# Expert choice: pooling the chosen tokens by rows fetched from DRAM instead of by products over all tokens

## The chip, the cores and the metric

The kernel runs on one core of one Trainium2 chip. The metric is device time in microseconds (us) of one execution; before the change it is 8233.12 us, the median of three runs (8232.96 to 8242.14).

The engines are named as in the profile: PE (TensorE matmul; PEld is its weight load), DVE (VectorE), ACT (ScalarE), POOL (GpSimd), SP (SyncE, which here only issues DMAs).

## The reference, cut to what matters

A network of four layers (each a token mixer and a feed-forward part) works on `x` of shape 4 x 128 x 64 x 64: four images of 4,096 tokens with 128 channels, all in float32. The change touches the feed-forward part of layers 1 and 2, an "expert choice" mixture of 64 experts in which each expert chooses its 8 best tokens of each image:

```
x = layernorm(tokens)                                   # over the 128 channels
logits = einsum('bsd,ed->bse', x, gate_w) + gate_b
probs = softmax(logits, axis=1)                         # over the 4,096 tokens
vals, idx = top_k(probs.transpose(0, 2, 1), 8)          # for each image and expert
gathered = take_along_axis(x, flat_idx)                 # the chosen tokens' rows
pooled = einsum('bked,bke->bed', gathered, topv)        # weighted sum of the 8 rows
h = gelu(einsum('ebd,edh->ebh', [pooled, 1], weight1))  # 128+1 -> 512
out = einsum('ebh,eho->ebo', [h, 1], weight2)           # 512+1 -> 128
outputs.at[b, flat_idx].add(topv * out)                 # back to the chosen tokens
```

The result is added to the tokens. Per layer, `weight1` and `weight2` hold 64 experts x 2 x 128 x 512 values, 32 MB.

## The kernel before

The whole `x` stays in SBUF as `xs`, 128 channels on the partitions, 4 images of 4,096 tokens along the free dimension. Eight phases run one after the other; `expert_choice(net, 1)` is the fourth and `expert_choice(net, 2)` the sixth. Between them lies a convolution, ahead of the first a deformable convolution, behind the second an attention.

On PE, ACT, DVE and POOL the instructions of a phase run in the order in which the program writes them (`manual_schedule(engines=ORDERED)`). SP is not among those: the order of its DMAs is set by the framework's planner, and each DMA waits for its data and for the buffer that it fills. A buffer pool that takes the place of another one waits for the old one's last users.

One expert stage has three parts.

Part A works on two pairs of images (`p` 0 and 1; the partitions hold 64 experts of the pair's first image and 64 of its second). `stat` makes the variances: a centring product of each chunk of 512 tokens, its square on ACT, and products that add the squares up. `scales` and `inverted` make the inverse deviations, and `turn_scales` transposes them so that each token's lies on its partition (`turned`). `logits` fills `chosen[p]`, 128 x 4,096. `largest` finds the eight largest of each row on DVE (MAX8), `exponentials` makes exp(logit - largest) and its sum (`totals`) on ACT. `choose` marks the eight places by overwriting them with a number (MATCH_REPLACE8) and then keeps the exponentials there and zero elsewhere; so `chosen[p]` becomes a sparse matrix of weights.

The pooling then takes 64 steps of 128 tokens. A step (`pool`, `gather`) transposes the 128 tokens of both images (two PE transposes, `moe_pt`), transposes the weights by a product with a diagonal matrix `diags[p]` that divides by the sum, brings the result to SBUF on ACT and DVE (`moe_tt`, with the tokens' scale `turned`), and adds the product of weights and tokens to `moe_acc`. `centre` takes the mean over channels off by one more product and writes `pooled`. The logits of pair 1 and its choice are interleaved with the first steps:

```
for n in range(PAIRS * NT):
    p, t = divmod(n, NT)
    tt = pool(p, t, p == 0 and t > 10)
    if before:
        gather(*before)
```

Part B goes through 16 groups of four experts: `first` (128 to 512), `turn` (transpose, bias, gelu), `second` (512 to 128), `hand` (collects the rows of all experts). A group's weights are two DMAs of 1 MB (`load`). Three groups' weights are fetched during part A into the pool `early`; the pool `late`, for two more, is opened when part A's pools are closed:

```
weights = [load(g) for g in range(EARLY)]
...
tc.tile_pool(name="moe_w_b", bufs=LATE) as late,
```

Part C multiplies the experts' results by `chosen` (64 products of 128 x 512) and adds them to `xs` on DVE.

The profile holds another phase that does what the change adds, in its own sizes. The deformable convolution writes rows of 512 bytes to a DRAM table (`dcn_table<-dcn_xt`, 64 partitions, 1,024 rows a DMA) and fetches rows of 2 KB by place, 128 for each indirect DMA (`dcn_g<-dcn_table,dcn_idx`). The involution writes zeros to the border of an image in DRAM (`inv_image<-inv_zero`): 128 rows of 1.8 KB a DMA, which don't start on round addresses.

Of the kernel before, what the change touches and what calls it, by code (L numbers as in the profile page):

```python
# [19 lines left out]
I32 = mybir.dt.int32  # L20
# [890 lines left out]
def expert_choice(net, layer):  # L911
# [9 lines left out]

    tc, nc, ins = net.tc, net.nc, net.ins
# [5 lines left out]
    PAIRS = B // 2  # L928
    EARLY, LATE = 3, 2
    GONE = -3.0e38  # L930
    w1, w2 = ins[f"L{layer}_ffn_weight1"], ins[f"L{layer}_ffn_weight2"]
    with ExitStack() as ctx:
        keep = ctx.enter_context(tc.tile_pool(name="moe", bufs=1))
# [11 lines left out]

        pooled = keep.tile([P, E, CG], F32, name="moe_pooled")
        nc.gpsimd.memset(pooled, 0.0)
        acts = [keep.tile([P, NH, EG, CG], F32, name=f"moe_act{i}") for i in range(2)]
        for t in acts:
            nc.gpsimd.memset(t, 0.0)  # L950
# [9 lines left out]
        cgate = keep.tile([D, E], F32, name="moe_cgate")  # L960

# [10 lines left out]
        with (  # L972
# [5 lines left out]
            def bank(tag, name):  # L978
                return ps.tile([P, CH], F32, name=f"moe_{name}", tag=tag, bufs=3 if tag in "ab" else 1)
# [3 lines left out]
            def stat(p, j):  # L983

                if j == 0:
                    stats[p] = (bank("pv", "pv"), [])
                pv, squares = stats[p]
                pd = bank("a", "pd")
                nc.tensor.matmul(pd, net.cent, net.chunk(2 * p + j // NCH, j % NCH), start=True, stop=True)
                sq = sb.tile([P, CH], F32, name="moe_sq", tag="moe_sq", bufs=6)  # L990
                nc.scalar.activation(sq, pd, AF.Square)
                squares.append(sq)
                if j % 4 == 1 and j > 4:
                    variances(p, j // 4 - 1)
# [56 lines left out]
            tops, exps, diags = {}, {}, {}  # L1051

            def largest(p):
                top = sb.tile([P, 8], F32, name="moe_top", tag="moe_top")
                nc.vector.max(out=top, in_=chosen[p])
                neg = sb.tile([P, 1], F32, name="moe_neg", tag="moe_neg")
                nc.vector.tensor_scalar_mul(neg, top[:, 0:1], -1.0)
                tops[p] = (top, neg)

            def exponentials(p):  # L1060
                exps[p] = sb.tile([P, N], F32, name="moe_exp", tag="moe_exp", bufs=1)
                nc.scalar.activation(exps[p], chosen[p], AF.Exp, bias=tops[p][1], accum_out=totals[p])

            def choose(p):
                lg = chosen[p]
                nc.vector.match_replace(out=lg, in_to_replace=tops[p][0], in_values=lg, imm_value=GONE)
                nc.vector.reciprocal(totals[p], totals[p])
                nc.vector.scalar_tensor_tensor(
                    out=lg, in0=lg, scalar=GONE, in1=exps[p], op0=ALU.is_equal, op1=ALU.mult
                )  # L1070
                diags[p] = sb.tile([P, P], F32, name="moe_diag", tag="moe_diag")
                nc.vector.tensor_scalar_mul(diags[p], net.ident, totals[p])

            accs = {}

            def pool(p, t, on_scalar):

                if t == 0:
                    accs[p] = bank("acc", "acc")[:, 0 : 2 * E]
                pt = bank("b", "pt")[:, 0 : 3 * P].rearrange("p (n c) -> p n c", c=P)  # L1080
                tok = slice(t * P, (t + 1) * P)
                for i in range(2):
                    nc.tensor.transpose(pt[:, 1 + i, :], net.xs[:, 2 * p + i, tok], net.ident)
                nc.tensor.matmul(pt[:, 0, :], chosen[p][:, tok], diags[p], start=True, stop=True)
                tt = sb.tile([P, 3, P], F32, name="moe_tt", tag="moe_tt", bufs=3)
                scale = turned[p][:, :, t // 4, t % 4]
                nc.scalar.copy(tt[:, 1:3, :], pt[:, 1:3, :])
                if on_scalar:
                    for i in range(2):
                        half = slice(i * E, (i + 1) * E)  # L1090
                        nc.scalar.activation(tt[:, 0, half], pt[:, 0, half], AF.Copy, scale=scale[:, i : i + 1])
                else:
                    nc.vector.tensor_mul(
                        tt[:, 0, :].rearrange("p (i e) -> p i e", e=E),
                        pt[:, 0, :].rearrange("p (i e) -> p i e", e=E),
                        scale.unsqueeze(2).to_broadcast([P, 2, E]),
                    )
                return tt

            def gather(p, t, tt):  # L1100
                for i in range(2):
                    half = slice(i * E, (i + 1) * E)
                    nc.tensor.matmul(
                        accs[p][:, half],
                        tt[:, 1 + i, :],
                        tt[:, 0, half],
                        start=t == 0 and i == 0,
                        stop=t == NT - 1 and i == 1,
                    )

            def centre(p):
                raw = sb.tile([P, 2 * E], F32, name="moe_raw", tag="moe_raw")
                nc.scalar.copy(raw, accs[p])
# [20 lines left out]
            for j in range(5):  # L1134
                stat(1, j)
            for c in range(NCH):
                logits(0, c)
            turn_scales(0)
            largest(0)
            for j in range(5, 10):  # L1140
                stat(1, j)
            exponentials(0)
            choose(0)
            for j in range(10, 2 * NCH):
                stat(1, j)
            scales(1)
            inverted(1)
            before = None
            for n in range(PAIRS * NT):
                p, t = divmod(n, NT)  # L1150
                tt = pool(p, t, p == 0 and t > 10)
                if before:
                    gather(*before)
                    if before[1] == NT - 1:
                        centre(before[0])
                before = (p, t, tt)
                if p == 0:
                    if 2 <= t < 2 + NCH:
                        logits(1, t - 2)
                    if t == 10:  # L1160
                        turn_scales(1)
                        largest(1)
                    if t == 17:
                        exponentials(1)
                        choose(1)
            gather(*before)
            centre(1)
# [3 lines left out]
        with (  # L1171
# [6 lines left out]
            def first(g):  # L1178
# [3 lines left out]
                ph = ps.tile([P, HID], F32, name="moe_ph", tag="ph")  # L1182
                for j in range(EG):
                    nc.tensor.matmul(
                        ph[j * CG : (j + 1) * CG], pooled[:, e0 + j, :], t1[:, j, :], start=True, stop=True
# [5 lines left out]
            def turn(g, hs):  # L1191
# [3 lines left out]
                for i in range(NH):  # L1195
                    nc.tensor.transpose(pt[:, i].rearrange("p j k -> p (j k)"), hs[:, i:HID:NH], net.ident)
                hid = sb.tile([P, NH, EG, B], F32, name="moe_hid", tag="hid")
                nc.vector.tensor_add(
                    hid,
# [3 lines left out]
                act = acts[g % 2]  # L1203
                nc.scalar.activation(act[:, :, :, 0:B], hid, AF.Gelu)
                return act

            def second(g, act, t2):
                po = ps.tile([P, D], F32, name="moe_po", tag="po")
                for i in range(NH):
                    for j in range(EG):  # L1210
                        nc.tensor.matmul(
                            po[j * CG : (j + 1) * CG],
# [8 lines left out]

# [727 lines left out]
```

## Time and profile before

| | us |
|---|---|
| median of three runs | 8233.12 |
| profiled execution | 8237.43 |
| its span (first to last instruction) | 8235.6 |
| stage of layer 1: first weight load to first product of the next phase | 2794.9 to 3056.3 |
| stage of layer 2: first DMA to first product of the next phase | 3375.8 to 3633.4 |

The mean granted clock of PE is 0.969 of full speed. The profile page gives busy time by engine, the span in 40 slices, the chain of work that ended last, and the costliest groups of instructions. Besides it, the trace answers for any stretch of the span: instructions in order of time, the chain in order of time, who waited for whom, busy time and granted clock by window, and DMA packets by window. Times in those lines are microseconds from the span's start; a line of the timeline has the start, the busy time, engine, line, operation, tiles, count, and in brackets the idle time before it with what ended it. "DMA share" is the mean busy share of the core's 16 DMA engines.

### The profile page before, as it was taken

Reading aid. Unit: us, or ns where it says so; the run is one execution under the profiler, and the core shown is the slowest. Engines: PE = TensorE matmul, PEld = TensorE weight load, DVE = VectorE, ACT = ScalarE, POOL = GpSimd, SP = SyncE. Lnnn points to the kernel's source line nnn. Section 1 sums busy time; section 2 is a strip of 40 time slices with the busy share of each in tenths; the row PEclk is TensorE's granted clock in tenths of the full one; section 3 lists DMA queues with packets and bytes.
Section 4 is the critical chain, followed back from the end, with each engine's and each line's share of the span. In section 5 each row is a group of like instructions: output and inputs, shape, how many; then the busy total and the mean of one; then the engine's idle time right before and its main releaser. Section 6 shows DMA issues by size and latency. Waiting matters only on the chain.

```text
span 8235.6 us, 146123 instructions
## 1 busy us (share of the span) xinstructions
PE 7626.6 (93%) x59726; PEld 3315.2 (40%) x59726; DVE 5525.9 (67%) x8715; ACT 3801.2 (46%) x7248; POOL 5253.5 (64%) x2925
## 2 busy tenths in 40 slices
PE   8999986777877889989999999999999999999899
PEld 2222243555555454443444344443444434444333
DVE  7888856888888632237767667766677667677155
ACT  4444433444444430323555555555555555555511
POOL 5989804777777400004888688887888878888700
PEclk9999998999999999988999999999999999999999
DMA  6434206877877430032554445544445445555400
GB/s 182 96 73 96 49 1 164 248 224 234 249 209 209 145 136 0 32 144 47 111 110 100 106 101 108 109 106 103 106 100 111 105 103 107 108 105 109 99 22 23
DMA packets 299127, 944.82 MB, mean 115 GB/s; under 512 B 41876, under 2 KB 114644, under 8 KB 240596
## 3 DMA queue, kind: packets, MB, share of 16 engines
q0 software_dynamic: 142848, 671.18, 34.6%
q1 hardware_dynamic: 155604, 264.26, 11.3%
q8 instruction: 469, 7.68, 0.4%
q14 instruction: 206, 1.69, 0.1%
HBM read 466.78 MB, written 65.88 MB: 65 GB/s over the span
## 4 chain that ended last, share of the span: by engine, by line
PE 57%; DVE 2%; issue 1%; DMA 1%; ACT 1%; POOL 0%; SPq 0%; DVEq 0%; ACTq 0%; POOLq 0%
PE att_pv L1552 15%; PE att_sc L1639 13%; PE att_mx L1496 11%; PE att_sc L1540 5%; PE conv_po L1306 3%; PE top_po L1852 3%; PE top_pw L1828 1%; DVE att_most L1507 1%; DMA moe_w<-in_L_ffn_weight 1%; PE att_sc L1469 0%; PE att_sc L1583 0%; PE top_po L1850 0%; PE att_sc L1600 0%; PE att_mx L1394 0%; PE att_sc L1430 0%
## 5 line engine op out<-in xcount | busy, mean ns | idle before, releaser
L1571 POOL TENSOR_TENSOR att_acc<-att_acc,att_ex 128x2048 f32<-128x2048 f32 x640 | 2902.0, 4534 | 638.5 <-ACT att_ex L1640 619.2
L1507 DVE TENSOR_REDUCE att_most<-att_mx 128x2 f32<-128x1024 f32 x2016 | 2461.8, 1222 | 1070.5 <-PE att_mx L1496 992.6
L1640 ACT ACTIVATE att_ex<-att_sc 128x512 f32<-128x512 f32 x4096 | 2222.9, 595 | 1771.4 <-PE att_sc L1639 1491.4
L1639 PE MATMUL att_sc<-att_q,att_k 32*128 32x512 f32 x8192 | 2455.7, 606 | 0.0
L1496 PE MATMUL att_mx<-att_k,att_q 32*128 32x512 f32 x8064 | 2292.2, 647 | 13.0 <-DVE att_parts L1519 10.8
L1540 PE MATMUL att_sc<-att_rows,att_ones_b 32*128 32x256 bf16 (+1 forms) x6144 | 1502.2, 306 | 4.7 <-ACT att_ex L1640 4.7
L816 POOL DMA_INDIRECT dcn_g<-dcn_table,dcn_idx x1152 | 1100.7, 955 | 436.9 <-DMA dcn_g<-dcn_table,dcn_idx 122.2
L1552 PE MATMUL att_pv<-att_ex,att_vals 128*32 128x256 f32 x16384 | 1309.8, 391 | 0.0
L1496 PEld LDWEIGHTS att_mx<-att_k,att_q 32*128 32x128 f32 x8064 | 610.9, 185 | 867.1 <-issue 707.6
L409 POOL TENSOR_TENSOR inv_prod<-inv_seen,inv_prod 128x512 f32<-128x512 f32 (+1 forms) x672 | 837.5, 1273 | 94.1 <-ACT inv_prod L408 94.1
L411 DVE SCALAR_TENSOR_TENSOR inv_prod<-inv_pk,bspan,inv_seen 128x512 f32<-128x512 f32 (+1 forms) x1120 | 774.6, 743 | 140.2 <-PE inv_pk L398 139.9
L1552 PEld LDWEIGHTS att_pv<-att_ex,att_vals 128*32 128x32 f32 x16384 | 322.5, 108 | 1318.9 <-issue 1300.8
L1639 PEld LDWEIGHTS att_sc<-att_q,att_k 32*128 32x128 f32 x8192 | 818.3, 183 | 10.7 <-issue 8.3
L830 ACT ACTIVATE dcn_one<-dcn_g,dcn_w 128x128 f32<-128x128 f32 x1152 | 457.5, 401 | 790.9 <-DMA dcn_g<-dcn_table,dcn_idx 787.6
L857 PE MATMUL dcn_pt<-ident,dcn_sum 128*128 128x128 f32 x2304 | 516.7, 308 | 242.6 <-DVE dcn_sum L841 241.8
L408 ACT ACTIVATE inv_prod<-inv_pk,bspan 128x512 f32<-128x512 f32 (+1 forms) x672 | 436.1, 682 | 503.8 <-PE inv_pk L398 503.8
L856 PE MATMUL dcn_pt<-ident,dcn_one 128*128 128x128 f32 x2304 | 482.9, 293 | 93.2 <-ACT dcn_st L873 81.1
L856 PEld LDWEIGHTS dcn_pt<-ident,dcn_one 128*128 128x128 f32 x2304 | 397.3, 203 | 305.7 <-issue 137.8
L398 PE MATMUL inv_pk<-inv_red,wtap 32*96 32x512 f32 (+1 forms) x3584 | 511.4, 636 | 7.4 <-DMA inv_seen<-inv_image 7.4
L857 PEld LDWEIGHTS dcn_pt<-ident,dcn_sum 128*128 128x128 f32 x2304 | 371.6, 203 | 322.1 <-DVE dcn_sum L841 321.0
L833 DVE TENSOR_SCALAR dcn_part<-dcn_g,dcn_w 128x128 f32<-128x128 f32 x1152 | 405.8, 352 | 122.5 <-DMA dcn_g<-dcn_table,dcn_idx 89.8
L420 PE MATMUL inv_out<-inv_prod,inv_fold 96*32 96x512 f32 (+1 forms) x3584 | 478.0, 605 | 8.5 <-DVE xs L428 8.5
(339 smaller groups left out, 7090.2 us busy)
## 6 DMA issues: line engine op xcount, KB each, us to landing
att_sum<-att_ex POOLq DMA_DIRECT2D x320, 1024.0 KB, 7.2
inv_seen<-inv_image SPq DMA_DIRECT2D x256, 266.0 KB
moe_w<-in_L_ffn_weight SPq DMA_DIRECT2D x64, 1024.0 KB
dcn_table<-dcn_xt SPq DMA_DIRECT2D x64, 512.0 KB
att_sum<-att_ex SPq DMA_DIRECT2D x32, 1024.0 KB
att_sum<-att_acc POOLq DMA_DIRECT2D x32, 1024.0 KB, 7.2
dcn_g<-dcn_table,dcn_idx POOLq DMA_INDIRECT x1152, 3.7
inv_image<-inv_rows SPq DMA_DIRECT2D x32, 304.0 KB
```

The lines of the kernel that those rows point to most:

```text
L409: nc.gpsimd.tensor_mul(of, view, of)
L411: nc.vector.scalar_tensor_tensor(out=of, in0=as_shape(pk[0:m], of), scalar=by, in1=view, op0=ALU.add, op1=ALU.mult)
L816: nc.gpsimd.indirect_dma_start(out=g, out_offset=None, in_=rows, in_offset=bass.IndirectOffsetOnAxis(ap=idx[:, j + i, k : k + 1], axis=0),)
L856: nc.tensor.matmul(out, one_, net.ident, start=i == 0, stop=False)
L857: nc.tensor.matmul(out, s, net.ident, start=False, stop=i == 3)
L1496: nc.tensor.matmul(pm[i] if alone else pm[:, i, :], q[r, t * P : (t + 1) * P], ks[r, kc * CH : (kc + 1) * CH], start=True, stop=True,)
L1507: nc.vector.tensor_reduce(most[:, 2 * half : 2 * half + 2, kc], pm, AX.X, ALU.max)
L1540: nc.tensor.matmul(pe[:, cols], ones_b[r], lows[g][r, cols], start=cols.start == 0, stop=False)
L1552: nc.tensor.matmul(block["pv"][r, cols], vals[b][:, t, r], ex[:, h, cols], start=t == 0 and half == 0, stop=t == NT - 1 and half == 1,)
L1571: nc.gpsimd.tensor_add(block["acc"], block["acc"], ex)
L1639: nc.tensor.matmul(pe, ks[r, t * P : (t + 1) * P], qs[c][r], start=False, stop=True)
L1640: nc.scalar.activation(ex[:, h, :], pe, AF.Exp)
```

## The change

The products over all tokens are taken out. In their place the tokens' rows are written to DRAM: `rows` transposes a chunk of 512 tokens of one image on PE, ACT copies it to `moe_xt`, POOL adds the tokens' scale as a 129th column, and SP writes 512 rows of 516 bytes to `moe_table`, one table for each pair of images. `largest` also finds the places of the eight largest (`max_index`), moves those of the second image up by 4,096 and turns them into integers. `ask` fetches the j-th chosen row of all 128 (image, expert) pairs by one indirect DMA on POOL. `pool` makes for each j a diagonal matrix of share times scale and adds up the eight rows by eight products with them; `centre`'s work stands at its end.

`choose` is split into `mark` and `choose`: pair 0's run during the second half of the rows, pair 1's during part B, since only part C needs them now. `turn_scales(0)` moves ahead of the logits, `exponentials(0)` behind `scales(1)`. `logits(1, ...)` are interleaved with the rows.

In part B, `pooled` and the activations hold four columns an expert instead of 32 with zeros between, and the PSUM tiles `phs` and `pos` are fixed and set to zero once by DVE. Two POOL memsets (`pooled`, `acts`) are gone.

```diff
+    K, ROW = 8, P + 1
+        tables = [dram.tile([2 * N, ROW], F32, name=f"moe_table{p}") for p in range(PAIRS)]
...
-        pooled = keep.tile([P, E, CG], F32, name="moe_pooled")
-        nc.gpsimd.memset(pooled, 0.0)
-        acts = [keep.tile([P, NH, EG, CG], F32, name=f"moe_act{i}") for i in range(2)]
-        for t in acts:
-            nc.gpsimd.memset(t, 0.0)
+        pooled = keep.tile([P, E, B], F32, name="moe_pooled")
...
+        def mark(p):
+            lg = chosen[p]
+            nc.vector.match_replace(out=lg, in_to_replace=tops[p], in_values=lg, imm_value=GONE)
+
+        def choose(p):
+            lg = chosen[p]
+            nc.vector.scalar_tensor_tensor(
+                out=lg, in0=lg, scalar=GONE, in1=exps, op0=ALU.is_equal, op1=ALU.mult
+            )
...
+            def rows(b, c):
+                p, i = divmod(b, 2)
+                pt = bank("b", "pt")
+                for t in range(4):
+                    tok = slice((4 * c + t) * P, (4 * c + t + 1) * P)
+                    nc.tensor.transpose(pt[:, t * P : (t + 1) * P], net.xs[:, b, tok], net.ident)
+                xt = sb.tile([P, 4, ROW], F32, name="moe_xt", tag="moe_xt", bufs=5)
+                nc.scalar.copy(xt[:, :, 0:P], pt.rearrange("p (t d) -> p t d", d=P))
+                nc.gpsimd.tensor_copy(xt[:, :, P], turned[p][:, i, c, :])
+                first = i * N + c * CH
+                nc.sync.dma_start(tables[p][first : first + CH, :].rearrange("(t p) r -> p t r", p=P), xt)
...
             def largest(p):
...
+                nc.vector.max_index(out=place, in_max=top, in_values=chosen[p])
+                row = sb.tile([P, K], F32, name="moe_row", tag="moe_row")
+                nc.vector.tensor_copy(row, place)
+                nc.vector.tensor_scalar(row, row, behind, None, op0=ALU.add)
+                places[p] = sb.tile([P, K], I32, name="moe_idx", tag="moe_idx")
+                nc.vector.tensor_copy(places[p], row)
...
+            def exponentials(p, neg):
+                nc.scalar.activation(exps, chosen[p], AF.Exp, bias=neg, accum_out=totals[p])
+                shares[p] = sb.tile([P, K], F32, name="moe_share", tag="moe_share")
+                nc.scalar.activation(shares[p], tops[p], AF.Exp, bias=neg)
+
+            def ask(p, j):
+                if j == 0:
+                    asked[p] = sb.tile([P, K, ROW], F32, name="moe_asked", tag="moe_asked")
+                nc.gpsimd.indirect_dma_start(
+                    out=asked[p][:, j, :],
+                    out_offset=None,
+                    in_=tables[p],
+                    in_offset=bass.IndirectOffsetOnAxis(ap=places[p][:, j : j + 1], axis=0),
+                )
+
+            def pool(p):
                 nc.vector.reciprocal(totals[p], totals[p])
+                nc.vector.tensor_scalar_mul(shares[p], shares[p], totals[p])
+                acc = bank("acc", "acc")[:, 0 : 2 * E]
+                for j in range(K):
+                    diag = sb.tile([P, P], F32, name="moe_diag", tag="moe_diag", bufs=4)
+                    nc.vector.tensor_scalar(
+                        diag, net.ident, shares[p][:, j : j + 1], asked[p][:, j, P : P + 1],
+                        op0=ALU.mult, op1=ALU.mult,
+                    )
+                    nc.tensor.matmul(acc, asked[p][:, j, 0:P], diag, start=j == 0, stop=j == K - 1)
...
+            turn_scales(0)
             for c in range(NCH):
                 logits(0, c)
-            turn_scales(0)
-            largest(0)
-            for j in range(5, 10):
-                stat(1, j)
-            exponentials(0)
-            choose(0)
-            for j in range(10, 2 * NCH):
+            neg = largest(0)
+            for j in range(5, 2 * NCH):
                 stat(1, j)
             scales(1)
+            exponentials(0, neg)
             inverted(1)
...
+            for n in range(2 * NCH):
+                rows(*divmod(n, NCH))
+                if n == 5:
+                    turn_scales(1)
+                if n > 5 and n % 2 == 0:
+                    logits(1, n // 2 - 3)
+            for n in range(2 * NCH):
+                rows(2 + n // NCH, n % NCH)
+                if n < 6 and n % 2 == 0:
+                    logits(1, 5 + n // 2)
+                if n == 5:
+                    neg = largest(1)
+                    mark(0)
+                    choose(0)
+                if 5 < n < 6 + K:
+                    ask(0, n - 6)
+            exponentials(1, neg)
+            for j in range(K):
+                ask(1, j)
+            pool(0)
+            pool(1)
...
+            phs = [ps.tile([P, HID], F32, name=f"moe_ph{i}", bufs=1) for i in range(2)]
+            pos = [ps.tile([P, D], F32, name=f"moe_po{i}", bufs=1) for i in range(2)]
+            for t in phs + pos:
+                nc.vector.memset(t, 0.0)
...
+                if g == 4:
+                    mark(1)
+                if g == 7:
+                    choose(1)
```

## The prediction

> **What bounds the kernel now.** I read the page first, then the chain of waits over the two expert stages, then windows inside them, then the DMA rows that come nearest to the new transfers.
>
> ```profile
> PE 7626.6 (93%) x59726; PEld 3315.2 (40%) x59726; DVE 5525.9 (67%) x8715; ACT 3801.2 (46%) x7248; POOL 5253.5 (64%) x2925
> ...
> PE 57%; DVE 2%; issue 1%; DMA 1%; ACT 1%; POOL 0%; SPq 0%; DVEq 0%; ACTq 0%; POOLq 0%
> ```
>
> The busiest engine by share and the chain agree on PE, but both average eight stages, most of them untouched here. The chain, cut to the second expert stage (layer 2), starts, lasts, what:
>
> ```profile
> 3421.96 0.59 PE moe_pr L1022 x4
> ...
> 3429.98 3.81 ACT moe_exp L1062 x2
> 3433.81 4.49 DVE moe_chosen L1066 x2
> 3438.37 4.39 DVE moe_chosen L1068
> 3442.96 3.26 DVE moe_rstd L1016
> ...
> 3535.44 0.49 PE moe_pc L1115 x2
> ...
> 3543.23 14.60 DMA moe_w<-in_L_ffn_weight
> ```
>
> The stage runs from 3375.8 to 3633.4 us and has three parts. Part A (statistics, logits, choice, pooling) ends with the centring product at 3535.9. Part B streams the 26 loads of 1,024 KB of weights that were not fetched earlier; the chain there is nearly all DMA. Part C adds the result to `xs` on DVE until 3633.4. Inside A, the exponentials, the marking, the choice and the reciprocal follow one another for 18 us while the token loop stands still. The same stage windowed (us, PE, PEld, DVE, ACT, POOL busy, granted clock, DMA share, GB/s):
>
> ```profile
> 3446.00:3476.00 30.00, 29.58 (x148) 14.39 (x148) 8.39 (x19) 12.77 (x25) 0.00 (x0) 0.87 0.00 1
> 3490.00:3536.00 46.00, 44.82 (x359) 41.72 (x358) 16.96 (x38) 21.95 (x70) 0.00 (x0) 0.95 0.01 1
> 3558.00:3574.00 16.00, 12.22 (x152) 7.31 (x152) 1.54 (x6) 2.53 (x6) 0.00 (x0) 0.89 1.05 406
> ```
>
> The first two windows are the token loop: PE is busy for nearly all of it, in 64 steps of three transposes or products and two small products. DMA is empty. In the third, DMA carries 406 GB/s and sets the pace. SP issues the first late weight load at 3535.96, when the centring product ends, so B can't start before A ends, and what A loses the whole stage loses. Layer 1 has the same shape: turning of the scales at 2841.8, centring ended at 2959.0.
>
> **The change, part by part (layer 2, then layer 1).** Removed: the loop from 3443 to 3535.9, less eight logits steps that stay. Added: 32 row blocks (four transposes, an ACT copy, a POOL column, a store of 512 rows of 516 B), 16 gathers, 16 diagonal products.
>
> *Until the rows.* The turning of the scales moves ahead of the logits at the same price. From 3422.5, PE has 11 statistics products of 0.93 us and four groups of variances of 1.0: 14.2, to 3436.7. No exponentials or DVE stand in it any more. ACT then takes the root (0.69), a table (1.28), the exponentials (3.71 + 0.19) and a small one (0.2): 3442.8. Copy 0.58, and 1.4 from issue to first data (the deformable stage's table stores were issued from 1275.96 and reached their rate near 1277.4): 3444.8.
>
> *The stores* are what I expect to bound the rows. The nearest rows are 512-byte stores of the deformable stage (1280 to 1315 us) and unaligned stores of 1.8 KB (24 to 28 us):
>
> ```profile
> DMA packets 12343, 6.24 MB, mean 178 GB/s; under 512 B 194, under 2 KB 12342, under 8 KB 12342
> ```
>
> ```profile
> DMA packets 885, 1.45 MB, mean 362 GB/s; under 512 B 97, under 2 KB 885, under 8 KB 885
> ```
>
> The first kept 97.4% of 16 engines busy: 0.974 x 35 x 16 / 12343 = 44 ns a packet. The second, 98.1%: 3.92 x 16 / 885 = 71 ns, or 80 if the 97 short packets are free; a line from 512 B (44) to the weights' 2 KB (81) gives 76 there, so starting off a boundary cost at most 4 ns. A 516-byte packet costs at least 44 and at most the 80 of the longer unaligned one; I take 47, by the nearer row. 16,384 x 47 / 16 = 48.1 us.
>
> [...]
>
> PE beside it: 29 more blocks of 0.86, eight logits of 2.01, 0.6 for the scales: 41.6, to 3484; covered by the stores. ACT has 32 x 0.58 and 8 x 1.3. The eight gathers of pair 0 share the engines: 65 gathers of 256 KB took 72.4% of 80 us (2700 to 2780), 0.89 us each; a quarter of the bytes costs 0.23 to 0.89, so 1.8 to 7.1, I take 3.5 (per-row costs don't shrink with the bytes). Stores end at 3444.8 + 48.1 + 3.5 = 3496.4, and land 1.0 later (the first table buffer's four stores ended near 1288.7, ACT was let go at 1289.7).
>
> *The tail.* `ask(1)` waits on POOL for the last store; nothing of the stage is queued behind it there. (`ask(0)` comes six blocks after its pair's last store and should find it landed; if not, the POOL columns of the last ten blocks queue behind it, and their stores on SP, which has only the late weight loads after them.) Its pace is in the first gathers of the deformable stage, and in ACT's wait for the first of them:
>
> ```profile
> 1331.70 1.22 POOL L816 DMA_INDIRECT dcn_g<-dcn_table,dcn_idx  x1 [83.39 <-DMA dcn_table<-dcn_zero]
> 1333.22 1.10 POOL L816 DMA_INDIRECT dcn_g<-dcn_table,dcn_idx  x1 [0.30 <-issue]
> 1334.63 0.95 POOL L816 DMA_INDIRECT dcn_g<-dcn_table,dcn_idx  x1 [0.30 <-issue]
> ```
>
> ```profile
> 1335.46 0.40 ACT L830 ACTIVATE dcn_one<-dcn_g,dcn_w 128x128 f32<-128x128 f32 x1 [4.28 <-DMA dcn_g<-dcn_table,dcn_idx]
> ```
>
> The eighth starts 1.52 + 1.41 + 5 x 1.25 = 9.2 after the first and lands 3.76 later: 13.0, to 3510.4. Diagonal 0.28, product 0.43, copy 0.27, centring 0.49, hops: 1.6, to 3512.0. Against 3535.9 that is 23.9 us. Layer 1 is the same 580.1 earlier: 2931.9 against 2959.0, 27.1. Sum 51.0.
>
> *The clock.* Today's stall is followed by PE at half speed; these are windows of layer 1 and layer 2:
>
> ```profile
> 2870.00:2880.00 10.00, 10.00 (x32) 4.15 (x28) 1.67 (x3) 2.84 (x6) 0.00 (x0) 0.50 0.00 0
> 3449.00:3452.00 3.00, 3.00 (x9) 0.58 (x8) 0.12 (x1) 0.58 (x1) 0.00 (x0) 0.50 0.00 0
> ```
>
> 0.50 lasted 14 us in layer 1 and 6 in layer 2: 7 + 3 us of PE time. The new wait for the exponentials is 4 to 6 us, about as long, and PE has little slack in the first 22 blocks. Between 0 and 10; I take 6.
>
> [...]
>
> *At nothing.* `max_index` (4.4 us as MATCH_REPLACE8, plus five small operations of 0.15) stands under 14 us of statistics on PE and ACT; bare, 5. `largest(1)`, `mark(0)`, `choose(0)` are 19 us on DVE from 3478, then 4.1 on ACT: 3501, with `pool(0)` behind it, before the last gathers at 3510; bare, 5. `mark(1)` and `choose(1)` delay DVE by 4.4 each in B, but five groups of weights are allocated, some 20 us of DMA queued; bare, 9. Four PSUM memsets (about 1.6) and fewer weight columns lie under the same stream. The POOL memsets removed were on no chain. B's 67 us of DMA and C don't change.
>
> Profiled time 8237.4 (span 8235.6 and 1.8 around it), less 45; the runs' median is 8233.1, so 8188. Ends: 44 ns, cheap gathers, no slow clock give 51 + 6 + 3.4 = 60, 8173; 56 ns (a quarter of the way from 47 to 80), dear gathers, 10 of clock give 51 - 18 - 7 - 10 = 16, 8217.
>
> **The rivals.**
> *PE-paced rows.* The 44 ns came from 64 partitions; if 128 store faster, PE sets the end at 3484, plus 4.2 to land, plus 14.6: 3503, and DVE's own chain holds it at 3506. Gain 30 + 33 - 6 = 57 or slightly more: 8174. Against it: the 1.8 KB stores, from 128 partitions, lie on the same line.
>
> *Dear stores (slower).* One mechanism: a 516-byte row costs what a long packet does, because it is cut in two or written in parts at both ends. At 80 ns, 33 x 1.024 = 33.8 more in each stage: 45 - 68 = -23, 8256. It decides from 47 + 22 = 69 ns, where the gain is zero. Against it: the involution's reads of 8.5 KB show as packets over 8 KB, not cut, and unaligned 1.8 KB cost 4 ns extra. For it: no row here has 516 B.
>
> *Slow clock throughout.* The deformable stage's transposes, waiting for stores as these would, ran at 0.57 to 0.60 between 1285 and 1305. At 0.72 (layer 1's slice from 2860 to 2890) the 41.6 us become 58, the stores land 7 later and the time is 8197; at 0.50 they become 83, 33 later, 8247; from 0.55 down there is no gain. Against it: PE is busy for 60% or more here, not 30%.
>
> That stores to one table queue behind each other's landing would cost 32 x 2 us a stage; the deformable stage stores to one table at 97% busy, which excludes it.
>
> **How the numbers follow.** Forecast 0.66 (0.06 of it within the band), PE-paced 0.12, dear stores 0.14 (0.03 within), slow clock 0.08 (0.03 faster, 0.02 within, 0.03 slower). 0.2% is 16.5 us and about what a measurement can tell from no change. Faster 0.60 + 0.12 + 0.03 = 0.75, same 0.06 + 0.03 + 0.02 = 0.11, slower 0.14. The range from 8168 to 8226 leaves out most of the dear stores and half of the slow clock.
>
> **What would show it.** Right: from the rows on, DMA near full at 165 to 185 GB/s for about 48 us, ACT or POOL waiting for `moe_xt` to land, POOL's last eight gathers 1.25 apart after the last store, the late weight loads 24 to 27 us sooner after the start of the stage, B unchanged at 406 GB/s. Wrong: DMA busy at 100 to 120 GB/s in the rows (dear stores), DMA half idle with PE at 0.5 (clock), or weight loads issued sooner but B longer.

## The result, and the profile after

The changed kernel takes 8199.67 us (median of 5 runs, 8194.69 to 8203.12) against 8234.96 for the kernel before in the same set: a ratio of 0.9951, 95% interval 0.9941 to 0.9962. The forecast of 8188, with a range of 8168 to 8226 and 0.75 on faster, holds, but the time lies 11.7 us above the forecast: 35.3 us were gained where 45 were said. The profiled span went from 8235.6 to 8197.9: 37.7 us, where the sum said 45.

Cut each expert stage at three marks that the trace has for both kernels: the first statistics product, the first late weight load on SP, and the first output product `moe_py`. Part A lies between the first two, part B between the last two.

| us | before, layer 1 / 2 | after, layer 1 / 2 | change |
|---|---|---|---|
| A | 163.3 / 159.4 | 141.3 / 137.0 | -22.0 / -22.4 |
| B | 76.8 / 77.0 | 80.1 / 81.6 | +3.2 / +4.6 |

A gave 44.4, B took 7.8 back, and everything else moved by 1.1. So there are two questions: what sets A now, and why a part that the diff hardly touches became longer.

The page's lines on busy time and on the chain of work that ended last show the average only: PE has 704 instructions fewer, and its share of the chain falls from 57% to 53%.

```profile
PE 7560.4 (92%) x59022; PEld 3232.8 (39%) x59022; DVE 5530.6 (67%) x8689; ACT 3768.7 (46%) x7100; POOL 5299.3 (65%) x3019
...
PE 53%; DVE 2%; issue 1%; DMA 1%; ACT 0%; POOL 0%; SPq 0%; POOLq 0%; DVEq 0%; ACTq 0%
```

The windows of layer 2 that answer to those of before (us, PE, PEld, DVE, ACT, POOL busy, granted clock, DMA share, GB/s): the first rows, the rows with logits beside them, the rows without, the weight stream.

```profile
3422.86:3434.86 12.00, 11.07 (x42) 6.53 (x44) 0.96 (x2) 6.55 (x15) 0.76 (x4) 0.57 0.95 153
3432.00:3452.00 20.00, 20.00 (x108) 9.03 (x108) 4.82 (x7) 13.35 (x25) 2.48 (x13) 0.97 0.84 167
3456.00:3470.00 14.00, 6.52 (x32) 4.31 (x32) 13.83 (x10) 5.07 (x9) 8.76 (x16) 0.66 1.11 177
3515.00:3545.00 30.00, 21.77 (x261) 11.24 (x254) 7.02 (x12) 4.22 (x11) 0.00 (x0) 0.88 1.05 386
```

In the first and third, DMA is near full (0.95 and 1.11) at 153 and 177 GB/s. In the second, where the logits run beside the rows, PE is full and DMA is at 0.84. In the third, PE is less than half busy; ACT waits 7.9 us in seven waits for the stores of `moe_xt` to land before it fills a buffer again, and POOL 3.1 us for ACT's copy. In the fourth the DMA share is what it was (1.05), but it carries 386 GB/s where it carried 406 or 407.

The chain over the end of A (start, lasts, what): the eight asks, the landing of the last, diagonal, centring, and then B's loads.

```profile
3479.67 0.97 POOL moe_asked L1108
...
3488.45 2.94 DMA moe_asked<-moe_table,moe_idx
...
3491.49 0.36 DVE moe_diag L1122
...
3493.04 0.81 PE moe_pc L1134 x2
...
3502.26 14.28 DMA moe_w<-in_L_ffn_weight
```

### The profile page after: what moved, and what is told of

Same layout as the page of the kernel before. It is cut to its first block, busy times and chain, and to the rows that moved or that the text cites. A ratio compares the mean times of both kernels' runs of the same rounds, so it can differ in the third digit from the quotient of the medians.

```text
span 8197.9 us, 144876 instructions
## 1 busy us (share of the span) xinstructions
PE 7560.4 (92%) x59022; PEld 3232.8 (39%) x59022; DVE 5530.6 (67%) x8689; ACT 3768.7 (46%) x7100; POOL 5299.3 (65%) x3019
## 4 chain that ended last, share of the span: by engine, by line
PE 53%; DVE 2%; issue 1%; DMA 1%; ACT 0%; POOL 0%; SPq 0%; POOLq 0%; DVEq 0%; ACTq 0%
PE att_pv L1576 15%; PE att_sc L1663 13%; PE att_mx L1520 11%; PE att_sc L1564 5%; PE top_po L1876 3%; PE top_pw L1852 1%; DVE att_most L1531 1%; DMA moe_w<-in_L_ffn_weight 1%; PE att_sc L1493 0%; PE att_sc L1607 0%; PE att_sc L1624 0%; PE top_po L1874 0%; PE att_mx L1418 0%; PE att_sc L1454 0%; PE att_sc L1520 0%
## 5 line engine op out<-in xcount | busy, mean ns | idle before, releaser
L1520 PE MATMUL att_mx<-att_k,att_q 32*128 32x512 f32 x8064 | 2292.1, 647 | 12.9 <-DVE att_parts L1543 10.8
```

Of the source, the lines that this page charges most:

```text
L1520: nc.tensor.matmul(pm[i] if alone else pm[:, i, :], q[r, t * P : (t + 1) * P], ks[r, kc * CH : (kc + 1) * CH], start=True, stop=True,)
```

## The experiments

Three sets of runs were made on three chips, each with the kernel before beside it (medians 8241.22, 8583.63 and 8235.37 us; the granted clock is about 0.935 on the second chip and 0.968 on the others), so a time stands only against others of its set. Part lengths come from each kernel's profile. "Rows" is the time from the first to the last packet of a layer's stores; rows and B, like A, are given for layer 1 and layer 2.

| kernel | set | A, layer 1 / 2 | rows | B | median | ratio to before, 95% |
|---|---|---|---|---|---|---|
| changed | first result | 141.3 / 137.0 | 53.4 / 52.5 | 80.1 / 81.6 | 8199.67 | 0.9951 (0.9941 to 0.9962) |
| before, shifted 32 B | 1 | 163.7 / 162.1 | none | 81.7 / 80.6 | 8245.03 | 1.0006 (0.9996 to 1.0015) |
| gap 416 B | 1 | 141.5 / 140.7 | 55.8 / 56.5 | 78.5 / 78.4 | 8198.00 | 0.9946 (0.9930 to 0.9963) |
| columns on ACT | 1 | 142.1 / 140.6 | 55.5 / 56.9 | 81.5 / 81.8 | 8207.13 | 0.9958 (0.9941 to 0.9974) |
| packed | 1 | 133.5 / 130.0 | 44.7 / 45.0 | 80.3 / 80.1 | 8179.91 | 0.9928 (0.9912 to 0.9945) |
| changed again | 2 | 134.8 / 131.6 | 49.5 / 47.3 | 80.0 / 81.6 | 8530.66 | 0.9938 (0.9924 to 0.9951) |
| gap 96 B | 2 | 134.8 / 133.4 | 48.7 / 49.2 | 81.8 / 80.1 | 8535.12 | 0.9938 (0.9923 to 0.9954) |
| three edits | 2 | 131.9 / 129.7 | 42.6 / 41.8 | 76.9 / 76.8 | 8525.67 | 0.9925 (0.9912 to 0.9939) |
| three, choice early | 2 | 128.9 / 128.9 | 43.6 / 43.6 | 76.6 / 76.5 | 8520.70 | 0.9918 (0.9905 to 0.9932) |
| gap 32 B | 3 | 135.6 / 132.6 | 49.1 / 48.1 | 81.5 / 80.1 | 8185.29 | 0.9938 (0.9923 to 0.9953) |
| split | 3 | 169.9 / 166.5 | 83.5 / 82.4 | 80.1 / 80.1 | 8254.69 | 1.0022 (1.0012 to 1.0031) |
| exponentials late | 3 | 131.2 / 130.1 | 51.8 / 50.0 | 80.3 / 80.0 | 8178.26 | 0.9932 (0.9917 to 0.9947) |
| five edits | 3 | 132.8 / 129.9 | 50.5 / 50.1 | 76.6 / 76.8 | 8173.50 | 0.9921 (0.9907 to 0.9934) |

**Why B grew.** The change adds tiles to the pool that lies ahead of the weight buffers in SBUF, and these begin at 139,360 bytes of a partition instead of 134,144: 96 past a multiple of 256 instead of on one. The rival: marking, choice and memsets, which the change put on DVE beside the stream, or the four-column operands. The first test spoils the kernel before, the second mends the changed one.

```
-        gbias = keep.tile([P, 1], F32, name="moe_gbias")
+        gbias = keep.tile([P, 9], F32, name="moe_gbias")[:, 0:1]
```

> The kernel before, with one unused gap of 32 bytes a partition ahead of the expert stage's weight buffers (they begin at 134,176 instead of 134,144 bytes of a partition); nothing else differs. Theory (the place of the weight buffers sets the rate): the late weight stream falls from 407 to about 386 GB/s, part B grows by about 3.5 us in each layer (from the first late load to the first output product 77.0 to 80.5), and the run by about 7 us. Rival (the rate is lost to DVE's marking and choice or to the diagonal products' shares that the change put beside the stream): 407 GB/s and 77.0 us as before, the run unchanged.

```
-        behind = keep.tile([P, 1], F32, name="moe_behind")
+        behind = keep.tile([P, 105], F32, name="moe_behind")[:, 0:1]
```

> The changed kernel, with one unused gap of 416 bytes a partition ahead of the weight buffers (they begin at 139,776 instead of 139,360 bytes; 139,776 is a multiple of 512 as 134,144 was). Theory (place): part B of layer 2 goes from 81.6 back to 77 to 78 us, its rate from 386 to 407 GB/s, and the run is about 7 us shorter than the changed kernel, near 8193. Rival (work beside the stream): 386 GB/s and 81.6 us stay, the run stays near 8200.

Windows of 16 or 30 us inside layer 2's stream, as the DMA view gives them: the kernel before, the changed one, the kernel before shifted, the changed one with the gap.

```profile
DMA packets 3263, 6.50 MB, mean 406 GB/s; under 512 B 103, under 2 KB 103, under 8 KB 3261
```

```profile
DMA packets 5813, 11.58 MB, mean 386 GB/s; under 512 B 174, under 2 KB 174, under 8 KB 5811
```

```profile
DMA packets 5818, 11.59 MB, mean 386 GB/s; under 512 B 175, under 2 KB 175, under 8 KB 5816
```

```profile
DMA packets 6135, 12.22 MB, mean 407 GB/s; under 512 B 181, under 2 KB 181, under 8 KB 6133
```

The rate goes with the address in both directions, whatever DVE does beside it: 16 x 16.00 us / 3263 = 78.5 ns a packet on a multiple of 256, 16 x 30 / 5813 = 82.6 off it. The place of the buffers is shown as the cause; the run's time alone would not have shown it (the interval around the shift's 1.0006 takes in no change, and the changed kernel itself did not run on the chip of the gap). Two gaps more ask how round the address must be; their edits are the same with 25 and 9 columns instead of 105.

> The changed kernel with a gap of 96 bytes ahead of the weight buffers: they begin at 139,456 bytes, a multiple of 64 but not of 128 (139,360 was 32 past a multiple of 64, 139,776 a multiple of 512). If multiples of 64 are enough: 407 GB/s and part B 78 to 79 us. If it takes 128 or more: 386 GB/s and 80 to 82 us.

> The changed kernel with a gap of 32 bytes: the weight buffers begin at 139,392 bytes, a multiple of 128 but not of 256 (64 past a multiple of 128 gave 386 GB/s, a multiple of 512 gave 407). If multiples of 128 are enough: 407 GB/s and part B 77 to 79 us. If it takes 256 or 512: 386 GB/s and 80 to 82 us. Part A as in the changed kernel; it is the one to hold the next kernels' parts A against.

Both ran at 386 to 387 GB/s. So four offsets past a multiple of 256 (32, 96, 128 and 192) cost the same: 82.4 to 82.6 ns a packet in windows of 30 us, 4 ns more than the 78.5 and 78.2 of the kernel before and the gap of 416. The rounded ones cost nothing (with 416 bytes the late buffers, by the sizes of the pools ahead of them in the source, lie 256 past a multiple of 512, and the stream has its 407 GB/s). The loss does not grow from 32 bytes to 192. What the 4 ns are is not shown.

The gap left B 1.4 to 1.7 us longer than before in the two layers of its run. The last `moe_ph` product starts 68.7 to 68.9 us after the first load in the kernel before and with the gap, and 72.0 to 72.1 in the changed kernel. From there to the first `moe_py` product it takes 8.1 or 8.2 us where the granted clock is 1.00, and 9.1 to 9.6 where it is 0.82 to 0.87, as with the gap: up to 1.5 us that come and go. Three later kernels with the same gap had the full clock there, and their B is 76.5 to 76.9, that of the kernel before.

**What sets the rows: POOL, the packets, or PE.** In the changed kernel POOL stood still while DVE made its choice for pair 0: two column copies, which take 0.19 us each elsewhere, took 4.43 together.

```profile
3469.84 4.43 POOL L1079 COPY moe_xt<-moe_turned 128x4 f32<-128x4 f32 x2
```

```profile
3469.67 4.42 DVE L977 SCALAR_TENSOR_TENSOR moe_chosen<-moe_chosen,moe_exp 128x4096 f32<-128x4096 f32 x1
```

I thought that this delayed the last two stores and with them the end of A.

```
-                nc.gpsimd.tensor_copy(xt[:, :, P], turned[p][:, i, c, :])
+                nc.scalar.copy(xt[:, :, P], turned[p][:, i, c, :])
```

> The changed kernel, with the 128x4 column of scales of each row block copied by ACT instead of POOL. Theory (POOL's copies stand still for the 4.4 us of the choice on DVE, and so the last two blocks' stores leave late and the last asks with them): no 4.4 us copy is left, the last store is issued 2 to 3 us sooner, the first late weight load 2 to 3 us sooner in each layer, the run 4 to 6 us shorter. Rival (the stores' packets on DMA set the end, and a store issued sooner only queues): the last store's landing and the first late load move by less than 0.7 us, the run by less than 1.5; ACT's 32 more copies of about 0.2 us may even cost it 1 to 2.

It didn't. Against the kernel with the gap of 416 bytes on the same chip, whose part A does the same work, A is 0.6 longer and 0.1 shorter (the run is 9.1 longer, 6.4 of it in B, which has the old place again). The last store is issued 0.4 and 1.7 us sooner after the stage's start, but its last packet ends 5.0 and 6.0 us after the issue instead of 3.0 and 4.0: it queues. The rival was right that A doesn't gain, though in layer 1 the last packet ended 1.6 us later after the stage's start, more than the 0.7 that it allowed.

```
-                    tok = slice((4 * c + t) * P, (4 * c + t + 1) * P)
+                    tok = slice(c * CH + t, (c + 1) * CH, 4)
...
-                nc.sync.dma_start(tables[p][first : first + CH, :].rearrange("(t p) r -> p t r", p=P), xt)
+                nc.sync.dma_start(tables[p][first : first + CH, :].rearrange("(p t) r -> p t r", p=P), xt)
```

(and `turn_scales` takes `rstds[p][:, k:CH:4]`)

> The changed kernel, with the tokens of a block dealt to partitions four in a row, so that a partition's part of a store is one run of 2,064 bytes in DRAM instead of four of 516 (the four transposes of a block read every fourth column of the activations; the table's content is the same). Theory (the packets of the stores set the pace of the rows from the 22nd block on): 128 packets a block instead of 512, DMA well below full in the rows, the rows end by PE or ACT, 6 to 13 us sooner in each layer, the run 12 to 25 us shorter, if the strided transposes cost no more than straight ones. Rival (PE at a low clock and the tail set the end): first late load sooner by less than 2 us in each layer. A third way: the runs of 2,064 bytes are cut up into packets of 512 or so again and nothing changes.

Windows with logits beside the rows, the kernel with the gap and then the packed one (columns as above):

```profile
3432.00:3452.00 20.00, 18.30 (x95) 7.09 (x94) 4.12 (x6) 12.86 (x24) 2.11 (x11) 1.00 1.18 159
```

```profile
3420.00:3440.00 20.00, 20.00 (x102) 8.77 (x100) 4.12 (x6) 13.46 (x25) 2.78 (x15) 1.00 0.42 157
```

The same GB/s at a third of the DMA share, and PE now without a gap. A packet of 2,064 bytes took 87 ns by its own time, with DMA far from full; for four of 516 the rows of that chip spent 4 x 54 to 56, gathers included. The rows are 11.1 and 11.5 us shorter, A is 8.0 and 10.8 shorter than with the gap alone, the run 18.1 us. The theory holds: on that chip the number of packets set the length of the rows.

```
-                nc.sync.dma_start(tables[p][first : first + CH, :].rearrange("(t p) r -> p t r", p=P), xt)
+                to = tables[p][first : first + CH, :].rearrange("(t p) r -> p t r", p=P)
+                nc.sync.dma_start(to[:, :, 0:64], xt[:, :, 0:64])
+                nc.sync.dma_start(to[:, :, 64:ROW], xt[:, :, 64:ROW])
```

> The changed kernel with each block's store as two, of 64 and of 65 columns: the same bytes in 32,768 packets of 256 and 260 bytes a stage instead of 16,384 of 516. This is the dear stores' mechanism (a row cut in two) made on purpose. By the packets measured so far (516 bytes 46 to 56 ns with the gathers, 2,064 bytes 87 ns: about 36 ns a packet and 0.025 ns a byte on the faster of the chips), 43 ns a packet: rows of 88 us instead of 50, part A 35 to 45 us longer in each layer, the run 70 to 90 us longer than the changed kernel and so slower than the kernel before. Rival (bytes alone count): the same rows within 3 us.

```profile
DMA packets 16401, 4.13 MB, mean 103 GB/s; under 512 B 16399, under 2 KB 16399, under 8 KB 16399
```

39 ns for half a row (16 x 40 / 16401) at 103 GB/s: the rows grow from 49.1 and 48.1 to 83.5 and 82.4 us, A by 34.2 and 34.0 against the gap of 32 bytes on the same chip, the run by 69.4, all just under what was expected, and the whole is slower than before at 1.0022. Twice the packets for the same bytes take 1.7 times as long: the bytes alone don't set the rows. It also prices the rival of dear stores: what it feared was 33.8 us a stage and 8256 us, and a row cut in two on purpose cost 34 and 8254.69.

> The changed kernel as it is, beside the others of this call on one chip. Part A took 141.3 us in layer 1 and 137.0 in layer 2; the variants that do the same there took 141.5 and 140.7. Theory (the stores' packets on DMA set the rows' end, at 51 to 56 ns a packet with the gathers, whatever TensorE's clock is): A of both layers between 137 and 142, and no longer where the rows begin at a lower clock. Rival (the clock after the stall sets it): A longer by 3 to 5 us in a layer whose first rows run at half clock than in one where they do not.

This was the changed kernel as it is. The theory's bounds didn't hold: A was 134.8 and 131.6. The rival was not put to the test, for the first rows of both layers ran at 0.86 and 0.88. What A does follow is the rows' time. Over the six kernels that store alike (the changed one twice, the three gaps, the columns on ACT), A of layer 2 less its rows is 83.7 to 84.5 us, while its rows range from 47.3 to 56.9. (In layer 2 of all of these A begins 68 us before the rows and ends 15 to 17 behind them, so that A can hardly differ by anything else.) By chip the rows' time over their packets is 46 to 48 ns in sets 2 and 3 (16 x 47.3 us / 16384 = 46.2) and 54 to 56 in set 1, gathers included. Why the chips differ in it, no run tells.

The clock's part is best seen inside one run, the first result: the first 12 us of the rows of layer 1 and of layer 2.

```profile
2866.10:2878.10 12.00, 12.00 (x60) 6.95 (x60) 1.64 (x3) 7.21 (x13) 0.96 (x5) 0.83 1.11 174
```

```profile
3423.82:3435.82 12.00, 12.00 (x45) 6.66 (x46) 0.96 (x2) 6.09 (x11) 0.95 (x5) 0.61 1.02 168
```

At 0.61 PE ran 45 matmuls instead of 60, but DMA was full in both (1.11 and 1.02), and the rows of layer 2 then took 52.5 us against 53.4. With the stores as they are, the low clock cost nothing that shows. It was also the exception: in the other eleven layers of those six kernels the same window has 0.83 to 0.89, by an estimate from these means 2.6 to 4.1 us at half speed ((1 - 0.83) x 12 / 0.5 = 4.1), and 9.4 in this one. Windows of 1 us in the first result agree: the clock is 0.50 from PE's first row at 2866.1 to 2870 in layer 1, and from 3423.8 to 3433 in layer 2. The prediction went by the 14 and 6 us of the kernel before; eleven of the twelve layers stayed below both.

```
-            exponentials(0, neg)
             inverted(1)
             for n in range(2 * NCH):
                 rows(*divmod(n, NCH))
+                if n == 4:
+                    exponentials(0, neg)
```

> The changed kernel with ACT's exponentials of pair 0 moved behind the fifth row block. Theory (the stores' packets set the end of part A, so every microsecond by which the first store leaves sooner ends it sooner; ACT's 4 us in the middle of the rows lie under five queued blocks of 1.5 us): the first store leaves 3.5 to 4.5 us sooner after the stage's start (67 to 63), part A is 3 to 4.5 us shorter in each layer, the run 6 to 9 us. Rival (TensorE's work and clock set the end of the rows, or ACT's 4 us stop them later): the first store leaves sooner, but part A is shorter by less than 1 us.

The first store left 6.6 and 3.6 us sooner after the stage's start than with the gap of 32 bytes, A fell by 4.5 and 2.5 (in layer 2 less than was expected), the run by 7.0. So two thirds of the head start arrive. For the rest, the window with the logits beside the rows points at PE in layer 2: it is full there at a granted clock of 0.99, and DMA is at 0.60.

```profile
3423.74:3441.74 18.00, 18.00 (x94) 7.27 (x92) 3.53 (x6) 13.04 (x24) 1.91 (x10) 0.99 0.60 161
```

**What is late next.** The gap of 416 bytes, the columns on ACT and the packed rows together:

> The changed kernel with three edits: the gap of 416 bytes, the scale columns on ACT, four tokens in a row on a partition. With packets no longer the bound, POOL's part was next: in the packed kernel its columns stood between the eight gathers of pair 0 and the last rows waited for them. Theory: the rows end 6 to 8 us sooner than in the packed kernel, the last eight gathers can start when their places are known (about 98 us after the stage's start instead of 115), but one of them is held for up to 4.4 us by the choice for pair 0 on DVE; A 124 to 128 us, B 78.5, the run 8164 to 8172. Rival (PE's 44 us of work in the rows is the bound after the packets, POOL only fills gaps): A as in the packed kernel, 130 to 133, the run 8175 to 8180.

The rival's figures were right: A is 131.9 and 129.7, its rows 42 us, near the 41.6 us of PE work that the prediction summed. Its reason holds for a part of the rows only, as two windows of layer 2 show:

```profile
3782.00:3788.00 6.00, 6.00 (x31) 2.63 (x32) 1.38 (x2) 4.37 (x12) 3.74 (x4) 1.00 0.53 157
3788.00:3794.00 6.00, 2.88 (x19) 2.29 (x18) 5.21 (x3) 3.14 (x9) 3.87 (x5) 0.90 0.85 231
```

PE is full from 3764 to 3788. From there to the last stores it is not; what the rows wait for there is not shown. Of the last asks, the first starts 1.4 to 1.8 us after the last store's last packet in all four kernels with packed rows. Here it took 4.79 us, starting 0.46 into DVE's choice; in layer 1 it took 4.46.

```profile
3803.34 4.79 POOL L1108 DMA_INDIRECT moe_asked<-moe_table,moe_idx  x1 [10.25 <-DVE moe_chosen L972]
```

```profile
3802.88 4.42 DVE L977 SCALAR_TENSOR_TENSOR moe_chosen<-moe_chosen,moe_exp 128x4096 f32<-128x4096 f32 x1
```

The next kernel only moves `mark(0)` and `choose(0)` from the second loop of rows to a place ahead of the first.

> The same three edits, and the marking and the choice for pair 0 moved on DVE ahead of the row blocks. Theory (the choice, a DVE instruction of 4.4 us with two operands in SBUF, holds whatever POOL does beside it): no gather of the last eight takes longer than 1.0 us (in the packed kernel the first took 4.81 and 2.05), and A is 3 to 4 us shorter than without this edit; the run 6 to 8 us shorter. Rival (the long first gather came from its own start or from the tables' landing): it stays at 2 to 5 us and A is the same within 1; the choice may even delay the logits of pair 1 by up to 4.

```profile
3801.93 0.95 POOL L1108 DMA_INDIRECT moe_asked<-moe_table,moe_idx  x1 [10.15 <-DMA moe_table<-moe_xt]
```

None of the last asks takes longer than 0.95 us now, in either layer, so the choice is shown to be what held it. A is 3.0 and 0.8 shorter: in layer 2 the rows end 3.2 us later, which takes most of the 4.0 that the asks gain. The run is 5.0 us shorter by the medians, with ranges that overlap.

The last kernel has the three edits and the late exponentials, and runs the logits of pair 1 four blocks sooner (so that marking and choice can be done by the last asks; the first asks move up with them).

> The changed kernel with five edits: the gap of 416 bytes, the columns on ACT, four tokens in a row on a partition, the exponentials of pair 0 behind the fifth block, and the logits of pair 1 four blocks sooner (so that the places, marking and choice on DVE are through before the last eight gathers). Theory: rows 4 us sooner, no gather held, A 123 to 127 us in each layer (129 to 132 for the three edits alone), B 77, the ratio to the kernel before 0.990. Rival (TensorE's work in the rows, 44 us at full clock, is the bound and starts no sooner): A 128 to 130, the ratio 0.992.

A is 132.8 and 129.9: the theory fails, and layer 1 lies above the rival's figure too. That is 1.6 longer and 0.2 shorter than with the late exponentials alone on the same chip. The first of the last asks still fell into the choice and took 2.22 and 2.30 us. The first store leaves 4 to 6.5 us sooner after the stage's start than in the kernels of three edits, but the rows last 50 us instead of 42 to 44. Windows at the exponentials and just behind them show where they stand, one of layer 1 and two of layer 2:

```profile
2864.00:2870.00 6.00, 2.28 (x10) 0.71 (x8) 0.86 (x2) 5.24 (x6) 0.00 (x0) 0.75 0.02 9
```

```profile
3409.29:3415.29 6.00, 5.96 (x22) 2.87 (x20) 0.15 (x1) 5.78 (x6) 0.00 (x0) 0.50 0.23 88
3415.29:3421.29 6.00, 6.00 (x20) 2.03 (x20) 1.40 (x3) 3.77 (x10) 0.00 (x0) 0.61 0.23 88
```

ACT is busy with the exponentials for 5.24 and 5.78 of 6 us, and DMA has little to move (9 and 88 GB/s): without packets that queue, ACT's work in the middle of the rows is no longer covered by them. In layer 1 PE stands idle behind it, in layer 2 it is busy at half its clock. The clock alone doesn't explain the longer rows: they last 50.5 us in layer 1, whose first 12 us have a granted clock of 0.99, and 50.1 in layer 2, where it is 0.68. That ACT's exponentials take what the head start gave is argued from these windows; no run separates them from the other four edits or from the clock.

Three edits with the early choice are the best ratio, 0.9918; they and the five edits beat both the kernel before and the changed one (each run of theirs is below each run of the changed kernel's copy in the same set, the plain one in set 2, the one with 32 bytes in set 3). Among themselves they can't be told apart.

## Why the prediction was right, and where its steps were not

**A, right as a sum.** It gave 44.4 of 45. By its own steps, layer 2 and then layer 1:
- *Until the rows*: first data at 69.0 us after the stage's start; measured 68.6, and in layer 1, where 69.8 was said, 71.9. "Layer 1 is the same 580.1 earlier" cost 2.1 us: that layer's stage began slower than before (granted clock 0.59 and 0.72 in its second and third five microseconds, 0.66 and 1.00 before), and I had taken its start as unchanged.
- *The stores*: 48.1 and 3.5 for the gathers, 51.6; measured 52.5 and 53.4. With the gathers 50.4 ns a packet was said; it was 51 and 52 here, 46 to 48 in two of the sets and 54 to 56 in the other. PE beside it was not all covered: it is full beside the logits (3432 to 3452), and with packed stores, where PE is full for more than half of the rows, they still last 42 to 45 us.
- *The tail*: 15.6 from the last packet to the first late load; measured 16.6 and 16.8. The asks took 8.8 (9.2 said) and stood 1.25 apart; the step between the stores' end and the first ask took 2.4 and 3.1 instead of 1.0. In layer 2 the last ask landed 2.9 after its start (3.8 said), and from there to the load it took 2.5 instead of 1.6.
- *The clock*: 6 us were taken off for it, and the two layers of this run show no cost of it in the rows. The 6 stood in for the 2.1 + 2.7 + 2.2 - 0.4 = 6.6 of the steps above. The sum was right by that exchange, which is luck, not by its reason.

**B, the step that failed.** "B's 67 us of DMA and C don't change" was sized at nothing and was 7.8: 3.3 in each layer by the buffers' place (68.7 to 72.0 and 68.8 to 72.1 up to the last `moe_ph` product), 1.3 in layer 2 by PE's clock behind it. I had asked what starting off a boundary costs the new rows (at most 4 ns, by the stores of 1.8 KB), and not where the new tiles would push the old buffers. With B as before, the sum would have come out at 45.5 of 45.

**At nothing.** The choice for pair 0 was put in the shade on DVE, and it was; that it stops POOL was not foreseen. In the changed kernel that still cost nothing that a run could show, because the packets came last. `max_index`, at 4.42 us, lay under the statistics as said, and the choice in B left the stream alone (407 GB/s from 3520 to 3550 in the kernel with the gap, whose choice for pair 1 runs from 3529.10 for 4.42 us).

**The rivals.** PE-paced rows (8174) is what packed stores make of it: 41.6 us said, 42 to 45 measured, though PE is not full to their end. Dear stores had its price right and its premise wrong: a row of 516 bytes is not cut (3432 to 3452: 3.34 MB in 6,633 packets, 202 of them under 512 bytes). A slow clock throughout didn't come: in layer 2 it is 1.00 from 3434 to 3458, and 0.66 from 3456 to 3470, where PE is less than half busy.

## What to carry to other kernels

Before a transfer that no edit touches is called unchanged, work out where its buffers will lie in SBUF: here 32 bytes ahead of them took a stream that sets the pace from 406 to 386 GB/s, 5%. For DRAM traffic in rows of some hundred bytes, count packets and not only bytes, and lay a partition's rows next to each other in DRAM so that they leave as one: here the rows took 82 to 84 us in packets of 256 and 260 bytes, 47 to 57 in packets of 516, and 42 to 45 in packets of 2,064 where ACT's exponentials stood ahead of them. When the last-ending wait is removed, look at once for the second: here the packets (rows of 47 to 57 us) and PE's work beside them (42) stood close to each other, with ACT's exponentials and POOL's asks behind them, and the edits together brought less than the sum of what each brought alone.

## What was not expected of the hardware

- On one core, weights of 2 KB a packet land at 406 to 407 GB/s in buffers on a multiple of 256 bytes of a partition (the kernel before, the gap of 416), and at 386 to 387 at offsets of 32, 96, 128 and 192 (the kernel before shifted, the changed one, the gaps of 32 and 96).
- The rows took 39 ns a packet and DMA engine in a full window of stores of 256 to 260 bytes (set 3), and 46 to 56 over all stores of 516, by the chip, gathers included. A packet of 2,064 bytes took 87 ns by its own time, with DMA not full, so its pace in a full queue is not shown.
- DVE's choice, with two operands in SBUF, held POOL's copies and its indirect DMA until it had ended (4.43 and 4.79 us); that it is the second operand that does it, is argued from the next sentence, and no run shows it by itself. Marking, maximum and index search, with one large operand each, held neither: beside them copies took 0.18 to 0.22 us and asks 0.94 to 0.99.
